# Scanning two states at a time on VectorE in a Mamba, attention and experts kernel

## The chip, the cores and the metric

The kernel runs on one core of one Trainium2 chip. The metric is the device time of one execution in microseconds (us); runs are compared by their medians. Five engines work side by side, each through its own queue in order: TensorE (PE in the profile, with its weight loads as PEld), VectorE (DVE), ScalarE (ACT), GpSimd (POOL) and SyncE (SP), which here only issues transfers.

## The reference

The input is `x` of shape (4, 128, 64, 64) in float32. Layer 0 normalises it by groups, then by channels, applies a 3x3 convolution per channel with a small residual branch, splits the 128 channels into four chunks of 32 and sends each through a Mamba block with 64 inner channels and 16 states per channel. A projection and a residual follow. Layer 1 is attention with four heads over the 4096 tokens of an image, then a choice of two out of eight experts per token. What matters here is the recurrence of the Mamba block:

```python
delta = jax.nn.softplus(dt @ dt_proj_w.T + dt_proj_b)
A = -jnp.exp(A_log)
dA = jnp.exp(delta[..., None] * A)
dBu = delta[..., None] * Bm[:, :, None, :] * xin[..., None]

def step(h, inp):
    dA_t, dBu_t, C_t = inp
    h = dA_t * h + dBu_t
    y = jnp.einsum('bdn,bn->bd', h, C_t)
    return (h, y)
```

For every image, inner channel and each of the 16 states n, h runs over the 4096 positions; y is the sum over n of C times h.

## The kernel before, in words

**Tiles.** An image is cut into 8 blocks of 512 positions (BLK). Two chunks of the 128 channels are handled together: 2 x 64 inner channels fill the 128 partitions. So an image has 8 blocks x 2 halves (index p) x 16 states (index n), and four images give 1024 units (b, i, p, n). Each is one state of one half block: a product `h = B * du`, a scan over 512 columns with the decay `da`, and a product `hc = C * h`, all on VectorE, in `scan` (L747 to L758). The scan begins at the value that the same state had at the end of the block before (`states`, L730), or at zero in the first block.

**The main loop** (L1244 to L1298) makes one unit per pass; a pass is called a slot. What it issues, in this order, on queues that keep the program's order (`Queue`, L439; all records so carry line 445):

1. `flush` issues stores that are due. Then the transfer that spreads B and C of the unit three slots on over the partitions (`fetched`, L732, tile `rows`, four buffers, 512 KB) from the DRAM tile `bcd`, which `inputs` (L679) wrote.
2. ScalarE copies the last column of the slot before's h into `states` (L1253), then makes the decay of the unit two slots on (`decayed`, L742, three buffers).
3. The next step of attention (`attention_groups`): TensorE makes the scores of two key tiles (`sc`), ScalarE their exponentials (`pT`).
4. VectorE's scan of the unit. In the first 128 slots (`ALONE`, L1241) its `hc` goes to the sum as it is. Later GpSimd adds the `hc` of an odd state to that of the even one (L1269) and the pair goes as one.
5. Two lanes of other work, X and Y, move on by two stages each (`advance`, L1158). A lane is a list of generators whose stages each issue a few instructions, so that normalisation, convolution, projections, the inputs of later scans (Y), the closing of a block (`closed`, L790) and the experts (`finished`, L1031) lie between scans. The order within the slot: second half of X's step, first of Y's, sums of `hc`, second of Y's, attention's weighted values of the slot before (`weighted`, TensorE tile `av`), first of X's.
6. The sum over states is made by TensorE in one PSUM buffer `y`: plain matmuls with the identity in the first 128 slots, later transposing matmuls (`turned_on`, L766), whose result ScalarE copies (`yT`) and TensorE turns back (`turned_back`, L781).

If a unit's inputs are not made in time, `until` (L1186) runs the lanes ahead. After the last scan the loop goes on with attention and experts alone. On image 0 the 3x3 convolution is done on TensorE, on later images on VectorE (`conv`, L609, tile `cm`).

Of the kernel before, what the change touches and what calls it, by code (L numbers as in the profile page):

```python
# [9 lines left out]
F32 = mybir.dt.float32  # L10
F32R = mybir.dt.float32r
# [25 lines left out]
def conv_mamba_attn_moe_kernel(ctx: ExitStack, tc: tile.TileContext, t: dict):  # L37
# [450 lines left out]
        return ps_work.tile(shape or [P, BLK], F32, tag=f"work{lane}", name=f"ps_{lane}")  # L488

    def tmp(lane, name, shape=None):  # L490
        return side.tile(shape or [P, BLK], F32, tag=f"tmp{lane}", name=name, bufs=4)

    def transposed(lane, src):
        ps = work(lane)
# [184 lines left out]
    def inputs(b, i, p):  # L679

        xn, pairs = xn_of[b, i], pairs_of[b, i]
        r = slice(DI * p, DI * p + DI)
        while held:
            yield
            yield
        held.add("in")
        ps = work("Y")
        summed(ps, [(inxc[:, j, :], pairs[:, p, 2 * j : 2 * j + BLK]) for j in range(2)])
        pz = work("X")
        mm(pz, inz[r, :], xn[r, 3 : 3 + BLK])  # L690
# [12 lines left out]
        held.clear()  # L703
        bc = tmp("Y", "bc")[0:DI, :]
        scalar.copy(bc, pb[0:DI, :])
        bcd = dram.tile([2, NST, 2 * BLK], F32, name="bcd", bufs=4)
        send(bcd.rearrange("c n (k q) -> (c n k) q", k=2), bc)

        e = tmp("Y", "e")
        scalar.activation(e, ps, AF.Abs, bias=dtb)  # L710
        scalar.activation(e, e, AF.Exp, scale=-1.0)
        ln = tmp("Y", "ln")
        scalar.activation(ln, e, AF.Ln, bias=1.0)
        delta = mix.tile([P, BLK], F32, name="delta", bufs=2)
# [17 lines left out]
    def fetched(b, i, p, n):  # L732

        bcd = in_of[b, i, p][4]
        w = mix.tile([P, 2, BLK], F32, name="rows", bufs=4)
        sync.dma_start(
            out=w.rearrange("p k q -> p (k q)"),
            in_=bcd[:, n, :][None].to_broadcast([DI, 2, 2 * BLK]),
        )
        return w  # L740

    def decayed(b, i, p, n):  # L742
        da = mix.tile([P, BLK], F32, name="da", bufs=3)
        scalar.activation(da, in_of[b, i, p][2], AF.Exp, scale=amat[:, n : n + 1])
        return da

    def scan(b, i, p, n, w, da):  # L747
# [12 lines left out]
    def scanned(b, i, p, y):  # L760
        xin, zs, delta, du, bcd = in_of.pop((b, i, p))
# [28 lines left out]
    def closed(b, i):  # L790
# [58 lines left out]
        for d, w, bias in ((kd, wkn, bkn), (qd, wqn, bqn)):  # L849
            ps = work("X")  # L850
            mm(ps, w, xa)
            yield
            hi = side.tile([P, BLK], F32R, name="hi", bufs=2)
            vector.tensor_scalar(hi, ps, bias, None, ALU.add)
            lo = side.tile([P, BLK], F32R, name="lo", bufs=2)
            vector.scalar_tensor_tensor(
                lo, ps, bias, hi.bitcast(F32), ALU.add, ALU.subtract
            )
            for half, w in enumerate((hi, lo)):
                w = w.bitcast(F32)  # L860
# [57 lines left out]
    def attention(b):  # L918
# [25 lines left out]
        for at, part in enumerate(parts):  # L944
# [9 lines left out]
            for g in range(0, NT * n, STEP):  # L954
# [9 lines left out]
                pTs = []  # L964
                for j in range(g, g + STEP):
                    sc = ps_sc.tile([P, 2, BLK], F32, name="sc")
                    for u in range(2):
# [4 lines left out]
                    pT = att.tile([P, 2, BLK], F32, name="pT", bufs=4)  # L972
                    scalar.activation(pT, sc, AF.Exp, scale=ATT_SCALE)
                    pTs.append((v[:, j // NT, j % NT, :], pT))
                yield (
                    b, q, h, pTs, first and g == 0, last and g + STEP == NT * n, prev, final,
                )

    sums, partial, total, inverse, later = [None], {}, {}, {}, deque()

    def weighted(group):
        b, q, h, pTs, first, last, prev, final = group
# [175 lines left out]
    def advance(lane, second):  # L1158
# [3 lines left out]
        while True:  # L1162
            if lane not in running:

                tasks = lanes[lane] if lanes[lane] or slot < len(units) else lanes["X"]
                if not tasks or not all(k in done for k in tasks[0][2]):
                    return False

                if (
                    tasks[0][0][0] == "out" and slot < len(units) + 4  # L1170
                    and not 2 <= slot % (2 * NST) < NST + 2
                ):
                    return False
# [68 lines left out]
    rows, decays, old, due, closing = {}, {}, None, deque(), deque()  # L1242
    even, y_of, waiting, slot = None, {}, None, 0
    while slot < len(units) or due or closing or waiting or left or later or lanes["X"] or running:  # L1244
        flush()

        for ahead in range(slot if slot == 0 else slot + 3, min(slot + 4, len(units))):
            until(("in", *units[ahead][:3]))
            rows[ahead] = fetched(*units[ahead])
        if old:  # L1250
            (b, i, p, n), h = old
            if i < NB - 1:
                scalar.copy(states[b % 2][:, p, n : n + 1], h[:, BLK - 1 : BLK])  # L1253
            old = None
        for ahead in range(slot if slot == 0 else slot + 2, min(slot + 3, len(units))):
            decays[ahead] = decayed(*units[ahead])
        group = next(groups, None)
        if slot < len(units):
            unit = units[slot]
            h, hc = scan(*unit, rows.pop(slot), decays.pop(slot))  # L1260
            old = unit, h
            b, i, p, n = unit
# [12 lines left out]
        while due and due[0][0] <= slot:  # L1275
            at, unit, term, first = due.popleft()
            b, i, p, n = unit
            if first:
                y_of[b, i, p] = ps_y.tile([P, BLK], F32, name="y")
            y, ends = y_of[b, i, p], n == NST - 1  # L1280
            if at <= ALONE:
                mm(y, ident, term, first, ends)
                if ends:
                    summed_up(b, i, p, y_of.pop((b, i, p)))
            else:
                turned_on(y, term, first, ends)
                if ends:
                    yT = mix.tile([P, BLK], F32, name="yT")
                    scalar.copy(yT, y_of.pop((b, i, p)))
                    closing.append((slot + 1, b, i, p, yT))  # L1290
        advance("Y", True)
        if waiting:
            weighted(waiting)
        waiting = group
# [31 lines left out]
def _laid_out(i):  # L1326
# [18 lines left out]
    wbc = np.zeros((P, 2, NST, 2), np.float32)  # L1345
    xdt, dtT = np.zeros((4, P), np.float32), np.zeros((4, P), np.float32)
    for c in range(2):
        d = slice(c, P, 2)
# [3 lines left out]
            inz[s, d] = c0["in_proj_w"][DI:].T  # L1352
            wout[d, p, s] = c0["out_proj_w"].T

        wbc[d, c] = c0["x_proj_w"][2:].reshape(2, NST, DI).transpose(2, 1, 0)
        xdt[2 * c : 2 * c + 2, d] = c0["x_proj_w"][:2]
        dtT[2 * c : 2 * c + 2, d] = c0["dt_proj_w"].T

# [53 lines left out]
```

## Time and profile before

| what | value |
| --- | --- |
| median of 3 runs | 5496.23 us (5489.41 to 5500.91) |
| the profiled execution's own time | 5490.03 us |
| its span in the trace | 5488.3 us |
| TensorE matmul busy | 4780.5 us, 87% |
| VectorE busy | 4404.5 us, 80% |
| ScalarE busy | 3923.3 us, 71% |
| GpSimd busy | 1981.4 us, 36% |
| 1024 scans | 1364.1 us (896 with a state) and 186.6 us (128 that begin at zero) |
| 1024 products h, 1024 products hc | 843.3 us and 882.4 us |

The profile is one execution recorded on the chip, with the start and length of each instruction. A group of instructions stands as engine, operation, tile written, tiles read and shape, followed by the count, the busy time in us, the mean in ns, the idle time of the engine just before them and what ended that idle time. Matmuls are pipelined, so that a busy TensorE is not a TensorE at its peak. Operations that can't start because another engine holds what they need may show this as a longer length, so a mean above the median is worth a look.

### The profile page before, as it was taken

The page shows a single profiled execution, that of the slowest core. Times are in us where ns is not written, and L with a number is a line of the kernel's source. Part 1 is how long each engine was busy: PE and PEld are TensorE (multiplying, and loading weights), DVE is VectorE, ACT ScalarE, POOL GpSimd, SP SyncE. Part 2 cuts the span into 40 slices and gives each one's busy share as a digit, 9 for nine tenths or more (in the row PEclk, how much of TensorE's full clock was granted, in tenths as well). Part 3 has the DMA queues.
Part 4 walks back from the last instruction along what each step waited for, and adds up shares of the span by engine and source line. Part 5 has one row for each costly group of instructions (what it writes and reads, how often), then busy time and mean ns, then how long its engine had stood idle before and what let it go on. Part 6 is the DMA issues. An engine that isn't in the chain of part 4 may idle for free.

```text
span 5488.3 us, 63616 instructions
## 1 busy us (share of the span) xinstructions
PE 4780.5 (87%) x18986; PEld 2159.0 (39%) x18986; DVE 4404.5 (80%) x6659; ACT 3923.3 (71%) x6045; POOL 1981.4 (36%) x1533
## 2 busy tenths in 40 slices
PE   4677798898988888898898898888889898999997
PEld 2223343443444443444444443344444443444443
DVE  4898888889888889988988888888989888871231
ACT  3455687788877777677877777777777777766553
POOL 2222345445433344344533434343443334420100
PEclk8778998999999999999999999999999999999998
DMA  3556566677656667666765666667765666765542
GB/s 98 173 178 195 194 216 229 223 233 254 219 197 206 226 206 244 221 225 220 252 214 196 221 209 233 237 202 240 250 207 200 209 225 196 249 200 167 168 148 68
DMA packets 451714, 1131.67 MB, mean 206 GB/s; under 512 B 51985, under 2 KB 135330, under 8 KB 451362
## 3 DMA queue, kind: packets, MB, share of 16 engines
q1 hardware_dynamic: 450194, 1126.74, 61.5%
q8 instruction: 153, 2.51, 0.2%
q14 instruction: 199, 1.63, 0.1%
q10 hardware_dynamic: 1168, 0.80, 0.1%
HBM read 967.12 MB, written 143.39 MB: 202 GB/s over the span
## 4 chain that ended last, share of the span: by engine, by line
PE 41%; DVE 31%; ACT 11%; issue 8%; DMA 7%; POOL 1%; SPq 0%; DVEq 0%; ACTq 0%; POOLq 0%
DVE h L445 17%; PE av L445 16%; PE sc L445 10%; PE ps_X L445 8%; PE ps_Y L445 5%; ACT pT L445 4%; DVE hc L445 3%; DMA ks<-kd 2%; PE y L445 2%; ACT xt L445 2%; DVE cm L445 2%; ACT L445 2%; DMA rows<-bcd 1%; DVE share L445 1%; DMA inv<-inverse 1%
## 5 line engine op out<-in xcount | busy, mean ns | idle before, releaser
L445 ACT ACTIVATE pT<-sc 128x1024 f32<-128x1024 f32 x2048 | 1983.1, 1022 | 976.0 <-PE sc L445 973.0
L445 PE MATMUL av<-pT,v 128*64 128x512 f32 x8192 | 2022.7, 615 | 7.3 <-ACT avs L445 7.1
L445 DVE TENSOR_TENSOR_SCAN h<-da,state,h 128x512 f32<-128x512 f32 x896 | 1364.1, 1522 | 100.7 <-ACT da L445 8.1
L445 PE MATMUL sc<-qs,ks 128*128 128x512 f32 x4096 | 1333.3, 447 | 116.1 <-ACT pT L445 60.1
L445 POOL TENSOR_TENSOR hc<-hc 128x512 f32<-128x512 f32 x448 | 677.6, 1513 | 1526.0 <-DVE hc L445 1354.4
L445 PEld LDWEIGHTS sc<-qs,ks 128*128 128x128 f32 x4096 | 728.1, 196 | 808.7 <-ACT pT L445 297.1
L445 DVE TENSOR_TENSOR hc<-rows,h 128x512 f32<-128x512 f32 x1024 | 882.4, 862 | 79.9 <-DVE h L445 2.7
L445 DVE TENSOR_TENSOR h<-rows,du 128x512 f32<-128x512 f32 x1024 | 843.3, 824 | 42.5 <-POOL du L445 25.6
L445 PEld LDWEIGHTS av<-pT,v 128*64 128x64 f32 x8192 | 506.0, 138 | 913.5 <-issue 880.9
L445 ACT ACTIVATE da<-delta,amat 128x512 f32<-128x512 f32 x1024 | 751.2, 734 | 16.7 <-DVE h L445 12.6
L445 ACT ACT_TABLE_LOAD x319 | 409.3, 1283 | 18.6 <-PE ps_Y L445 13.3
L445 POOL TENSOR_TENSOR rsY<-rsY,mhalf 128x4 f32<-128x4 f32 x100 | 139.9, 1399 | 575.1 <-DVE shiftY L445 574.1
L445 ACT COPY state<-h 128x1 f32<-128x1 f32 x896 | 177.2, 198 | 221.8 <-DVE h L445 221.4
L445 POOL TENSOR_TENSOR avs<-avs,prev 128x512 f32<-128x512 f32 x96 | 145.1, 1511 | 425.3 <-ACT avs L445 343.3
L445 PE MATMUL y<-ident,hc 128*128 128x128 f32 x1792 | 274.9, 277 | 7.0 <-POOL hc L445 7.0
L445 PEld LDWEIGHTS y<-ident,hc 128*128 128x128 f32 x1792 | 223.1, 142 | 106.4 <-issue 50.4
L445 DVE TENSOR_TENSOR share<-share,xf 128x1024 f32<-128x1024 f32 x128 | 174.5, 1363 | 105.0 <-DMA share<-sharesX 73.9
L445 PE MATMUL ps_X<-share,w_ew 128*128 128x512 f32 x432 | 224.4, 643 | 39.4 <-DVE share L445 39.4
L445 POOL TENSOR_TENSOR rsX<-rsX,mhalf 128x4 f32<-128x4 f32 x92 | 112.3, 1221 | 304.7 <-DVE shiftX L445 304.3
L445 POOL TENSOR_SCALAR du<-e 128x512 f32<-128x512 f32 x64 | 128.3, 2005 | 251.5 <-ACT e L445 251.5
L445 POOL TENSOR_TENSOR zs<-xin,zs 128x512 f32<-128x512 f32 x64 | 107.4, 1678 | 290.1 <-DVE xin L445 280.9
L445 PE MATMUL y<-hc,ident 128*128 128x512 f32 x256 | 169.4, 758 | 45.5 <-DVE hc L445 45.3
(239 smaller groups left out, 4832.2 us busy)
## 6 DMA issues: line engine op xcount, KB each, us to landing
rows<-bcd SPq DMA_DIRECT2D x1024, 512.0 KB
ks<-kd SPq DMA_DIRECT2D x192, 512.0 KB
qs<-qd SPq DMA_DIRECT2D x161, 512.0 KB
share<-sharesX SPq DMA_DIRECT2D x108, 512.0 KB
v<-vd SPq DMA_DIRECT2D x192, 256.0 KB
ks<-kd SPq DMA_DIRECT2D x128, 256.0 KB
avd<-avs SPq DMA_DIRECT2D x96, 256.0 KB
prev<-avd SPq DMA_DIRECT2D x96, 256.0 KB
```

The source lines that it names most:

```text
L445: return lambda *args, **kw: queued(op(*args, **kw))
```

## The change

A unit is now two neighbouring states, and there are 512 of them. It takes two slots, so that the number of slots and what the lanes and attention do in each stay what they were.

- The scan runs over one row of 1025 columns: 512 of the first state, one column between them, 512 of the second. In the column between, the decay is a constant zero (written once into two standing decay tiles), and the driving term is the second state's value from the block before. The recurrence so forgets the first state and begins at that value. ScalarE writes it there (`carried`). The initial value of the scan is always read from `states`, which GpSimd fills with zeros at the start of each image.
- In the even slot VectorE makes the product `h` of both states (1024 columns, `driven`) and the scan. In the odd slot, after lane X's step, it makes the product `hc` of both (`read`).
- `bcd` is laid out so that a fetched tile holds B of both states or C of both, not B and C of one. The count and the size of the transfers stay. C of the next unit is fetched in the even slot and B of the unit after it in the odd one.
- A unit's decays are made one in each of the two slots before it. ScalarE saves both last columns with one copy at the end of the even slot (`kept`).
- The first 64 slots, not 128, send `hc` to the sum without GpSimd's addition; there, too, the transposing form is used. Buffers: two of h and hc with both states in each, two of the decay.
- The two halves `hi` and `lo` of keys and queries use lane X's common temporaries, now six. The exponentials are issued by a function of their own at the same place.

```diff
@@
-        return side.tile(shape or [P, BLK], F32, tag=f"tmp{lane}", name=name, bufs=4)
+        return side.tile(
+            shape or [P, BLK], F32, tag=f"tmp{lane}", name=name, bufs=6 if lane == "X" else 4
+        )
@@
-        bcd = dram.tile([2, NST, 2 * BLK], F32, name="bcd", bufs=4)
-        send(bcd.rearrange("c n (k q) -> (c n k) q", k=2), bc)
+        bcd = dram.tile([2, NST // 2, 2, 2 * BLK], F32, name="bcd", bufs=4)
+        send(bcd.rearrange("c n k (m q) -> (c n k m) q", m=2), bc)
@@
+    decays = [mix.tile([P, 2, BLK + 1], F32, name=f"da{k}") for k in range(2)]
+    for k in range(2):
+        gpsimd.memset(decays[k][:, 0, BLK:], 0.0)
...
+    def carried(unit):
+
+        b, i, p, n = unit
+        if (i, p, n) == (0, 0, 0):
+            gpsimd.memset(states[b % 2], 0.0)
+        h = mix.tile([P, 2, BLK + 1], F32, name="h", bufs=2)
+        scalar.copy(h[:, 0, BLK:], states[b % 2][:, p, n + 1 : n + 2])
+        return h
+
+    def kept(unit, h):
+        b, i, p, n = unit
+        if i < NB - 1:
+            scalar.copy(states[b % 2][:, p, n : n + 2], h[:, :, BLK - 1])
+
+    def driven(unit, h, w):
+        b, i, p, n = unit
         du = in_of[b, i, p][3]
-        h = mix.tile([P, BLK], F32, name="h", bufs=3)
-        vector.tensor_mul(h, w[:, 0, :], du)
+        vector.tensor_mul(h[:, :, 0:BLK], w, du[:, None, :].to_broadcast([P, 2, BLK]))
+
+    def scan(unit, h, da):
+
+        b, i, p, n = unit
+        h, da = (a.rearrange("p k q -> p (k q)")[:, 0 : 2 * BLK + 1] for a in (h, da))
         vector.tensor_tensor_scan(
-            out=h, data0=da, data1=h, initial=0.0 if i == 0 else states[b % 2][:, p, n : n + 1],
+            out=h, data0=da, data1=h, initial=states[b % 2][:, p, n : n + 1],
             op0=ALU.mult, op1=ALU.add,
         )
-        hc = mix.tile([P, BLK], F32, name="hc", bufs=5)
-        vector.tensor_mul(hc, w[:, 1, :], h)
-        return h, hc
+
+    def read(h, w):
+        hc = mix.tile([P, 2, BLK], F32, name="hc", bufs=2)
+        vector.tensor_mul(hc, w, h[:, :, 0:BLK])
+        return hc
@@
-    units = [(b, i, p, n) for b, i in blocks for p in range(2) for n in range(NST)]
-
-    ALONE = NB // 2 * 2 * NST
...
+    units = [(b, i, p, n) for b, i in blocks for p in range(2) for n in range(0, NST, 2)]
+    END = 2 * len(units)
+
+    ALONE = NB // 2 * NST
...
+        fetch((at + 2, 0) if odd else (at + 1, 1))
+        unit = units[at] if at < len(units) else None
+        prepared(at + 1, odd)
         group = next(groups, None)
+        if group:
+            group = exponentials(group)
+        if unit and not odd:
+            h = h_of.pop(at)
+            driven(unit, h, rows.pop((at, 0)))
+            scan(unit, h, decays[at % 2])
+        advance("X", True)
+        if unit and odd:
+            hc = read(h, rows.pop((at, 1)))
             if slot < ALONE:
-                due.append((slot + 1, unit, hc, n == 0))
-            elif n % 2 == 0:
-                even = hc
+                due.append((slot + 1, unit, 0, hc[:, 0, :], False))
+                due.append((slot + 2, unit, 1, hc[:, 1, :], ends(unit)))
             else:
-                gpsimd.tensor_add(even, even, hc)
-                due.append((slot + 2, unit, even, n == 1))
-        advance("X", True)
+                gpsimd.tensor_add(hc[:, 0, :], hc[:, 0, :], hc[:, 1, :])
+                due.append((slot + 2, unit, 0, hc[:, 0, :], ends(unit)))
         advance("Y", False)
...
         advance("Y", True)
+        if unit and not odd:
+            kept(unit, h)
         if waiting:
             weighted(waiting)
         waiting = group
```

Here `prepared(ahead, k)` makes decay k of a unit and, with the second one, its carry.

More of the change, by code (lines that the diff above doesn't have):

```diff
@@ L730, in conv_mamba_attn_moe_kernel, with fetched @@
     states = [mix.tile([P, 2, NST], F32, name=f"state{k}") for k in range(2)]
-    def fetched(b, i, p, n):
-        bcd = in_of[b, i, p][4]
+    decays = [mix.tile([P, 2, BLK + 1], F32, name=f"da{k}") for k in range(2)]
+    for k in range(2):
+        gpsimd.memset(decays[k][:, 0, BLK:], 0.0)
+    def fetched(unit, k):
+        b, i, p, n = unit
         w = mix.tile([P, 2, BLK], F32, name="rows", bufs=4)
         sync.dma_start(
-            out=w.rearrange("p k q -> p (k q)"),
-            in_=bcd[:, n, :][None].to_broadcast([DI, 2, 2 * BLK]),
-        )
-        return w
@@ L742, in decayed @@
[L742 to L747, printed above, removed]
+            out=w.rearrange("p m q -> p (m q)"),
+            in_=in_of[b, i, p][4][:, n // 2, k, :][None].to_broadcast([DI, 2, 2 * BLK]),
+        )
+        return w
+    def decayed(unit, da, k):
+        b, i, p, n = unit
+        scalar.activation(
+            da[:, k, 0:BLK], in_of[b, i, p][2], AF.Exp, scale=amat[:, n + k : n + k + 1]
+        )
@@ L749, in scan @@
+    def carried(unit):
[10 more added lines that the diff above has]
+    def driven(unit, h, w):
+        b, i, p, n = unit
         du = in_of[b, i, p][3]
-        h = mix.tile([P, BLK], F32, name="h", bufs=3)
@@ L751, in scan @@
-        vector.tensor_mul(h, w[:, 0, :], du)
+        vector.tensor_mul(h[:, :, 0:BLK], w, du[:, None, :].to_broadcast([P, 2, BLK]))
+    def scan(unit, h, da):
+        b, i, p, n = unit
+        h, da = (a.rearrange("p k q -> p (k q)")[:, 0 : 2 * BLK + 1] for a in (h, da))
         vector.tensor_tensor_scan(
-            out=h, data0=da, data1=h, initial=0.0 if i == 0 else states[b % 2][:, p, n : n + 1],
+            out=h, data0=da, data1=h, initial=states[b % 2][:, p, n : n + 1],
             op0=ALU.mult, op1=ALU.add,
@@ L852, in closed @@
             yield
[L853 to L858, printed above, removed]
+            hi, lo = tmp("X", "hi"), tmp("X", "lo")
+            vector.tensor_scalar(hi.bitcast(F32R), ps, bias, None, ALU.add)
+            vector.scalar_tensor_tensor(lo.bitcast(F32R), ps, bias, hi, ALU.add, ALU.subtract)
             for half, w in enumerate((hi, lo)):
-                w = w.bitcast(F32)
                 if len(d.shape) == 4:
@@ L963, in attention @@
                         ahead = load(nxt, qs if nxt[:2] == (q, h) and not nxt[5] else None)
-                pTs = []
+                scs = []
                 for j in range(g, g + STEP):
@@ L971, in attention, with exponentials @@
                         )
-                    pT = att.tile([P, 2, BLK], F32, name="pT", bufs=4)
-                    scalar.activation(pT, sc, AF.Exp, scale=ATT_SCALE)
-                    pTs.append((v[:, j // NT, j % NT, :], pT))
+                    scs.append((v[:, j // NT, j % NT, :], sc))
                 yield (
-                    b, q, h, pTs, first and g == 0, last and g + STEP == NT * n, prev, final,
+                    b, q, h, scs, first and g == 0, last and g + STEP == NT * n, prev, final,
                 )
     sums, partial, total, inverse, later = [None], {}, {}, {}, deque()
+    def exponentials(group):
+        pTs = []
+        for v, sc in group[3]:
+            pT = att.tile([P, 2, BLK], F32, name="pT", bufs=4)
+            scalar.activation(pT, sc, AF.Exp, scale=ATT_SCALE)
+            pTs.append((v, pT))
+        return *group[:3], pTs, *group[4:]
     def weighted(group):
@@ L1163, in advance @@
             if lane not in running:
-                tasks = lanes[lane] if lanes[lane] or slot < len(units) else lanes["X"]
+                tasks = lanes[lane] if lanes[lane] or slot < END else lanes["X"]
                 if not tasks or not all(k in done for k in tasks[0][2]):
@@ L1169, in advance @@
                 if (
-                    tasks[0][0][0] == "out" and slot < len(units) + 4
+                    tasks[0][0][0] == "out" and slot < END + 4
                     and not 2 <= slot % (2 * NST) < NST + 2
@@ L1238, in conv_mamba_attn_moe_kernel @@
     groups = attention_groups()
-    units = [(b, i, p, n) for b, i in blocks for p in range(2) for n in range(NST)]
-    ALONE = NB // 2 * 2 * NST
-    rows, decays, old, due, closing = {}, {}, None, deque(), deque()
-    even, y_of, waiting, slot = None, {}, None, 0
-    while slot < len(units) or due or closing or waiting or left or later or lanes["X"] or running:
-        flush()
[L1247 to L1256, printed above, removed]
-        group = next(groups, None)
[L1258 to L1262, printed above, removed]
+    units = [(b, i, p, n) for b, i in blocks for p in range(2) for n in range(0, NST, 2)]
@@ new lines, in conv_mamba_attn_moe_kernel, with fetch, prepared @@
+    END = 2 * len(units)
+    ALONE = NB // 2 * NST
+    rows, due, closing, y_of = {}, deque(), deque(), {}
+    h_of, slot = {}, 0
+    def fetch(*wanted):
+        for ahead, k in wanted:
+            if ahead < len(units):
+                until(("in", *units[ahead][:3]))
+                rows[ahead, k] = fetched(units[ahead], k)
+    def prepared(ahead, k):
+        if ahead < len(units):
+            decayed(units[ahead], decays[ahead % 2], k)
+            if k:
+                h_of[ahead] = carried(units[ahead])
@@ new lines, in ends @@
+    def ends(unit):
+        return unit[3] == NST - 2
+    waiting = None
+    while slot < END or due or closing or waiting or left or later or lanes["X"] or running:
+        at, odd = divmod(slot, 2)
+        flush()
+        if slot == 0:
+            fetch((0, 0), (0, 1), (1, 0))
+            prepared(0, 0)
+            prepared(0, 1)
+        fetch((at + 2, 0) if odd else (at + 1, 1))
+        unit = units[at] if at < len(units) else None
+        prepared(at + 1, odd)
+        group = next(groups, None)
+        if group:
[7 more added lines that the diff above has]
+            hc = read(h, rows.pop((at, 1)))
@@ L1275, in conv_mamba_attn_moe_kernel @@
         while due and due[0][0] <= slot:
-            at, unit, term, first = due.popleft()
-            b, i, p, n = unit
+            _, (b, i, p, n), k, term, done_with = due.popleft()
+            first = n == 0 and k == 0
             if first:
                 y_of[b, i, p] = ps_y.tile([P, BLK], F32, name="y")
[L1280 to L1290, printed above, removed]
+            turned_on(y_of[b, i, p], term, first, done_with)
+            if done_with:
+                yT = mix.tile([P, BLK], F32, name="yT")
+                scalar.copy(yT, y_of.pop((b, i, p)))
+                closing.append((slot + 1, b, i, p, yT))
         advance("Y", True)
+        if unit and not odd:
+            kept(unit, h)
         if waiting:
@@ L1344, in _laid_out @@
     wout = np.zeros((P, 2, P), np.float32)
-    wbc = np.zeros((P, 2, NST, 2), np.float32)
+    wbc = np.zeros((P, 2, NST // 2, 2, 2), np.float32)
     xdt, dtT = np.zeros((4, P), np.float32), np.zeros((4, P), np.float32)
@@ L1353, in _laid_out @@
             wout[d, p, s] = c0["out_proj_w"].T
-        wbc[d, c] = c0["x_proj_w"][2:].reshape(2, NST, DI).transpose(2, 1, 0)
+        wbc[d, c] = c0["x_proj_w"][2:].reshape(2, NST // 2, 2, DI).transpose(3, 1, 0, 2)
         xdt[2 * c : 2 * c + 2, d] = c0["x_proj_w"][:2]
```

## The prediction

> **What bounds the kernel now.** I read the shares of busy time first, because two engines compete for the bound, and then the chain that ended last.
>
> ```profile
> PE 4780.5 (87%) x18986; PEld 2159.0 (39%) x18986; DVE 4404.5 (80%) x6659; ACT 3923.3 (71%) x6045; POOL 1981.4 (36%) x1533
> PE 41%; DVE 31%; ACT 11%; issue 8%; DMA 7%; POOL 1%; SPq 0%; DVEq 0%; ACTq 0%; POOLq 0%
> ```
>
> The reader sees that neither TensorE (PE) nor VectorE (DVE) is the bound alone. An average hides stages, so next I took busy time by stretch. Scans start between 97.5 us (first) and 4895.7 us (last). One pass of the main loop, a slot, holds one scan. In the trace scan 128 starts at 577.4 and scan 288 at 1282.9 us, so the four rows are slots 0 to 127 (stage A), 128 to 287 (B), 288 to 1023 (C) and the tail without scans (D). Columns: length, PE, PEld, DVE, ACT, POOL busy, clock, DMA share, GB/s.
>
> ```profile
> 97.50:577.40 479.90, 350.77 (x842) 138.66 (x843) 420.00 (x603) 265.22 (x489) 125.12 (x105) 0.79 0.55 183
> 577.40:1282.90 705.50, 616.96 (x2499) 277.96 (x2499) 616.90 (x821) 555.80 (x854) 324.35 (x236) 0.94 0.66 220
> 1282.90:4895.70 3612.80, 3225.42 (x13354) 1484.17 (x13352) 3192.95 (x4683) 2767.32 (x4281) 1471.84 (x1107) 0.96 0.66 222
> 4895.70:5488.30 592.60, 547.72 (x2184) 239.30 (x2180) 150.31 (x425) 310.49 (x384) 41.94 (x44) 0.95 0.41 136
> ```
>
> A slot takes 3.75, 4.41 and 4.91 us in A, B and C. VectorE's 4.34 us of C is not all of its load: about 0.1 us in front of every scan and 0.08 in front of every hc product is idle time with almost no releaser named (70.4 + 7.2 + 57.8 us in C, 0.18 us per slot), the step from a result to its reader. With that VectorE is taken 3.48, 4.04 and 4.52 us per slot, TensorE 2.74, 3.86 and 4.38. A is VectorE's, C is nearly shared. In C each waits for the other; the waits of C:
>
> ```profile
> DVE res L445 <- PE ps_X L445: 106.6, 40, 7.0
> PE ps_X L445 <- DVE aT L445: 75.6, 21, 5.6
> PE ps_X L445 <- DVE prX L445: 65.4, 18, 4.6
> ACT state L445 <- DVE h L445: 73.0, 49, 3.0
> ```
>
> TensorE's lane work waits for VectorE's lane work that stands behind the scan in VectorE's queue. So VectorE's time is worth something in C, but not one for one.
>
> Last, the scan itself, one unstalled state, and the stalls (start, length):
>
> ```profile
> 2613.14 0.69 DVE L445 TENSOR_TENSOR h<-rows,du 128x512 f32<-128x512 f32 x1
> 2613.93 1.28 DVE L445 TENSOR_TENSOR_SCAN h<-da,state,h 128x512 f32<-128x512 f32 x1
> 2615.25 0.69 DVE L445 TENSOR_TENSOR hc<-rows,h 128x512 f32<-128x512 f32 x1
> 2615.86 0.74 DVE L445 TENSOR_SCALAR hi<-ps_X,w_bqn 128x512 fp32r<-128x512 f32 x1
> ...
> 2602.56 1.61 POOL L445 TENSOR_TENSOR hc<-hc 128x512 f32<-128x512 f32 x1 [0.95 <-DVE hc L445]
> 2603.13 2.13 DVE L445 TENSOR_TENSOR_SCAN h<-da,state,h 128x512 f32<-128x512 f32 x1
> ```
>
> From start to start one state occupies 0.79 + 1.32 + 0.61 = 2.72 us. A scan that meets a running GpSimd add takes 2.13 instead of 1.28 us. Medians and means of the three groups, and of the one operation with 1024 columns that the kernel already has:
>
> ```profile
> L445 DVE TENSOR_TENSOR_SCAN h<-da,state,h x896: 1282/1284/2395, 201.2 to 4895.7; 128x512 f32<-128x512 f32 x180
> L445 DVE TENSOR_TENSOR h<-rows,du x1024: 621/684/1784, 96.7 to 4894.9; 128x512 f32<-128x512 f32 x171
> L445 DVE TENSOR_TENSOR share<-share,xf x128: 1211/1221/2001, 1426.9 to 5479.7; 128x1024 f32<-128x1024 f32 x128
> L445 DVE TENSOR_TENSOR hc<-rows,h 128x512 f32<-128x512 f32 x1024 | 882.4, 862 | 79.9 <-DVE h L445 2.7
> ```
>
> (The first three give shortest, median and longest ns; the last busy us and the mean, 862 ns against a median of 693, so the difference is stalls.)
>
> **What the Trainium skill says.** "VectorE: DVE Perf Modes", the section on the perf-mode tier table: an fp32 product of two SBUF tensors runs at one element per cycle, with no faster mode. The trace agrees: 512 further columns cost 1221 - 684 = 537 ns. "DVE: opcode table, instruction layouts, handler registers and perf-mode slots", section 6: the built-in scan runs at half that throughput. The trace fits: 1284 ns is 2 x 537 plus 210 fixed. "SBUF — State Buffer", section "Who interferes with whom": a VectorE operation with two SBUF inputs and a GpSimd operation that reads SBUF exclude each other for the whole instruction. The 2.13 us scan above agrees. "Trainium Kernel Development and Optimization", section "Performance Expectations", warns that matmul busy time is a bad measure of how full TensorE is; so 4.38 us may overstate it, which I keep as a rival.
>
> **The change part by part.** *VectorE.* Two states take 2 x 2.72 = 5.44 us now. The new h product costs 0.79 + 0.54 = 1.33, the new hc product 0.61 + 0.54 = 1.15. No scan of 1025 columns is in the trace. Lower end: 513 more columns at two cycles, 513 x 2 x 1.049 = 1.08, so 1.32 + 1.08 = 2.40; upper end: no fixed part at all, 2.64. Nothing says that it gets below the lower end, whose fixed part is inferred from the product. I take 2.40, since its rate is what the page states. Sum 4.88, a saving of 0.56 us per pair, 0.28 per slot (0.16 at the upper end). The zero column is the 1025th and costs nothing else. The products' layout (a row pitch of 513) is not in the trace; I bound hc between 1.15 and the old 2 x 0.61, and take 1.15.
>
> *Stalls.* The pairwise GpSimd add stays, one per pair from slot 128 on, and each can hold one VectorE operation for some 0.85 us. Fewer but longer operations could meet it more or less often; bounds plus or minus 0.1 us per slot, value zero. But the bound ALONE falls from 128 to 64 slots: slots 64 to 127 get 32 GpSimd adds that they did not have, 32 x 0.85 = 27 us of VectorE in stage A.
>
> *ScalarE.* 896 state copies of 198 ns become 448 two-column ones plus 512 carries: 64 more, 13 us, beside the 23% of C in which ScalarE is idle (2767 of 3613 us busy); zero. Without that cover it would cost those 13 us. Two-column copies are not in the trace (198 to 396 ns); still hidden. The wait of the copy for the scan comes once per pair, in the even slot. Queued behind it are the second decay, the carry and the next exponentials, for which TensorE's score buffers wait. The decay has 0.73 us of work and the whole hc product in the odd slot ahead of its scan: no cost taken, up to 0.1 us per slot as bound.
>
> *TensorE and the y sum.* 128 plain 512-column products in A become transposing ones plus eight turns back, on an engine busy 73% of A: zero. In the first 64 slots the next y's first term now stands right behind the turn back in the single y buffer, and waits for VectorE to read it: four times, some 3 us (a scan and a product), 10 us at most with half of it hidden; I take 6.
>
> *DMA.* The row fetches stay 1024 of 512 KB, one per slot, three slots ahead of use, on SP's queue in the same place. A fetch into a reused buffer waits for the last product that read it: the h product for B rows, the hc product for C rows, both in the slot before, as now; zero. The send of bcd keeps size and place. hi and lo, and the position of the exponentials, move no instruction on an engine's queue; zero.
>
> *What becomes of it.* A: 128 x 0.28 = 36 less 27 less 6 = 3 us. B: VectorE falls to 4.04 - 0.28 = 3.76, under TensorE's 3.86. Today a slot is 0.37 us longer than its fuller engine; that stays, so 3.86 + 0.37 = 4.23, and 160 x 0.18 = 29 us. C: VectorE falls to 4.24, TensorE's 4.38 is next. Overhang 4.91 - 4.52 = 0.39, slot 4.77, and 736 x 0.14 = 103 us. D: no scans, zero. Sum 135 us. The profiled execution took 5490.03 us, its span 5488.3; it becomes about 5355. The median of the runs shown is 6 us above it, so I name 5361.
>
> **The rivals.** *VectorE's time counts in full.* For it: TensorE's busy time may be inflated, and in C TensorE waits for aT, prX and share products. Against it: the 106.6 us for which VectorE waits for ps_X. Then 896 x 0.28 = 251 plus 3, giving 5242.
>
> *It is mostly absorbed.* TensorE is already the bound in most slots, or the scan comes out at its upper end (0.16 per slot). Half of B and C: 66 us, giving 5430; less with stalls, to 5480.
>
> *Slower: bunched VectorE work holds TensorE in even slots.* Now 2.72 us plus stalls stand before each slot's lane work; then 1.33 + 2.40 = 3.73 in the even slot and nothing before lane X in the odd one. That is 1.0 us more in the even slot. If all of it reaches the in-order TensorE queue, and the odd slot can give back only TensorE's present slack, 4.91 - 4.38 = 0.53, a pair loses 0.47: 368 x 0.47 = 173 less 32 gives about 5640. It decides once more than 0.53 of that 1.0 us arrives at TensorE. Against it: VectorE has only 1.15 us of scan work in the odd slot and can start the next pair early.
>
> **How the numbers follow.** Forecast, 5300 to 5420: 0.50. In full, 5230 to 5300: 0.15. Absorbed, 5420 to 5485: 0.17. Within 0.2% (11 us, about what a measurement of this kernel can tell from no change): 0.04. Slower: 0.14. So faster 0.82. The range 5240 to 5470 leaves out the slower case, no change and the rim of the absorbed one, about 0.2. Both ends hold the bounds above: the stalls' 0.1 us is 90 us over B and C.
>
> **What would show it.** Right: 512 scans near 2.4 us median and about 1.22 us for both products; VectorE busy near 4404 - 250 to 290; slots of C near 4.77 us; the tail still about 590 us; waits of ps_X for aT and prX smaller, those of VectorE for ps_X larger. Wrong: scan or products with longer medians, means much above the medians (stalls grew), idle time of ScalarE in front of the state copy above 150 us, or TensorE waiting for lane X work in even slots.

## The result and the profile after

The changed kernel takes 5487.11 us at the median of 14 runs (5472.36 to 5493.63), the kernel before 5497.68 us in the same rounds (5486.38 to 5508.94). The ratio is 0.9982, its 95% interval 0.9974 to 0.999. That is 10 us, where 135 were forecast. The profiled execution took 5488.16 us, its span 5486.3.

VectorE's work fell by more than forecast, yet the time stayed. Part 1 of the page after:

```profile
PE 4717.2 (86%) x19146; PEld 2166.4 (39%) x19146; DVE 4014.9 (73%) x5123; ACT 3932.9 (72%) x6117; POOL 2416.2 (44%) x1571
```

VectorE is busy 390 us less (4404.5 before), in 1536 fewer instructions. The same four stretches, cut at the scans of the same slots (columns as before):

```profile
99.70:583.60 483.90, 283.30 (x990) 152.87 (x990) 395.21 (x412) 263.95 (x498) 215.59 (x137) 0.71 0.54 182
583.60:1283.60 700.00, 613.38 (x2508) 278.06 (x2507) 542.07 (x581) 557.17 (x870) 378.57 (x237) 0.95 0.66 222
1283.60:4890.80 3607.20, 3229.64 (x13351) 1476.05 (x13348) 2899.91 (x3578) 2775.50 (x4327) 1760.76 (x1109) 0.96 0.66 222
4890.80:5486.30 595.50, 550.82 (x2190) 240.50 (x2188) 152.76 (x425) 311.22 (x384) 42.97 (x45) 0.95 0.41 136
```

Stage A takes 4 us more, B 5.5 less, C 5.6 less, the tail 3 more. In C VectorE gives up 293 us of work and the slot falls from 4.91 to 4.90 us. The three operations (shortest, median and longest ns):

```profile
L445 DVE TENSOR_TENSOR h<-rows,du x512: 1206/1220/2323, 98.3 to 4889.5; 128x1024 f32<-128x1024 f32 x171
L445 DVE TENSOR_TENSOR_SCAN h<-da,state,h x512: 2353/3172/3457, 99.7 to 4890.8; 128x1025 f32<-128x1025 f32 x171
L445 DVE TENSOR_TENSOR hc<-rows,h x512: 1154/1220/2318, 102.1 to 4894.2; 128x1024 f32<-128x1024 f32 x171
```

Unstalled, the operations are as long as the forecast took them: the shortest long scan has 2353 ns, and the products' median is 1220. But most long scans were held up: their median is 3172 ns. What grew besides is VectorE's idle time for lane X, and with it TensorE's for `lo` and `share`. (In lane X, `hi` and `lo` are the halves of keys and queries, `stX` the statistics of a normalisation, `prX` the router's scores, `share` an input of the experts and `res` their sum; `ps_X` is what TensorE hands over.) Some of the waits in stage C of the changed kernel (us in total, times, longest):

```profile
DVE res L445 <- PE ps_X L445: 130.2, 54, 3.9
DVE stX L445 <- PE ps_X L445: 109.9, 23, 4.9
DVE hi L445 <- PE ps_X L445: 98.9, 20, 6.8
DVE prX L445 <- PE ps_X L445: 48.8, 22, 3.9
PE ps_X L445 <- DVE share L445: 62.7, 28, 3.9
PE ps_X L445 <- DVE lo L445: 62.5, 23, 3.0
```

In C before, `res` waited 106.6 us, and `hi` and `prX` do not stand in VectorE's list of the nine longest. The others, before:

```profile
DVE stX L445 <- PE ps_X L445: 43.1, 22, 2.0
PE ps_X L445 <- DVE share L445: 39.4, 24, 2.2
PE ps_X L445 <- DVE lo L445: 24.0, 25, 1.6
```

TensorE's waits in C for `aT` and `prX` fell, as the forecast had it, from 75.6 to 31.0 and from 65.4 to 3.9 us, 106 us together. But those for `share`, `lo`, ScalarE's `xt` and GpSimd's `hc` rose by 110 us. So TensorE stood idle for 378 us of C, where it had been 387.

How a wait for lane X works is seen in one place of the time line. In the kernel before, VectorE first, then TensorE:

```profile
2606.80 0.72 DVE L445 TENSOR_TENSOR h<-rows,du 128x512 f32<-128x512 f32 x1
2607.62 1.28 DVE L445 TENSOR_TENSOR_SCAN h<-da,state,h 128x512 f32<-128x512 f32 x1
2608.94 1.59 DVE L445 TENSOR_TENSOR hc<-rows,h 128x512 f32<-128x512 f32 x1
2610.46 0.74 DVE L445 TENSOR_SCALAR hi<-ps_X,w_bkn 128x512 fp32r<-128x512 f32 x1
```

```profile
2601.91 1.24 PE L445 MATMUL ps_X<-ident,xt 128*128 128x128 f32 x4
...
2607.21 1.13 PE L445 MATMUL ps_X<-xa,w_wkn 128*128 128x512 f32 x2 [0.48 <-ACT xa L445]
...
2617.44 1.16 PE L445 MATMUL ps_X<-w_wv,xa 128*128 128x128 f32 x8 [1.49 <-DVE lo L445]
```

VectorE does a state's three operations while `ps_X` is made, and `hi` begins without idle time. The same place of the same block in the changed kernel:

```profile
2597.60 1.21 DVE L445 TENSOR_TENSOR h<-rows,du 128x1024 f32<-128x1024 f32 x1
2598.92 2.36 DVE L445 TENSOR_TENSOR_SCAN h<-da,state,h 128x1025 f32<-128x1025 f32 x1
2606.93 0.75 DVE L445 TENSOR_SCALAR hi<-ps_X,w_bkn 128x512 fp32r<-128x512 f32 x1 [5.66 <-PE ps_X L445]
...
2608.39 1.32 DVE L445 TENSOR_TENSOR hc<-rows,h 128x1024 f32<-128x1024 f32 x1
...
2613.09 2.35 DVE L445 TENSOR_TENSOR_SCAN h<-da,state,h 128x1025 f32<-128x1025 f32 x1
2615.36 0.72 DVE L445 TENSOR_SCALAR hi<-ps_X,w_bqn 128x512 fp32r<-128x512 f32 x1
2616.11 0.75 DVE L445 SCALAR_TENSOR_TENSOR lo<-ps_X,w_bqn,hi 128x512 fp32r<-128x512 f32 x1
```

```profile
2599.46 1.48 PE L445 MATMUL ps_X<-ident,xt 128*128 128x128 f32 x4 [0.29 <-ACT xt L445]
...
2605.77 1.12 PE L445 MATMUL ps_X<-xa,w_wkn 128*128 128x512 f32 x2 [0.39 <-ACT xa L445]
...
2616.92 0.58 PE L445 MATMUL ps_X<-w_wv,xa 128*128 128x128 f32 x1 [2.95 <-DVE lo L445]
```

The scan ends at 2601.28. VectorE's next instruction in the odd slot is lane X's `hi`, whose input TensorE makes from 2605.77 on. So VectorE stands still for 5.66 us, though the hc product behind `hi` has had all it needs since 2601.28. That product, the next h product and the next scan then come late, the next `hi` and `lo` stand behind them, and now TensorE waits 2.95 us. The time saved on VectorE is spent in idle time in front of one instruction, and a later instruction is late all the same.

### The profile page after: what moved, and what is told of

The parts are those of the page before. It is cut to its first block, busy times and chain, and to the rows that moved or that the text cites. A ratio compares the mean times of both kernels' runs of the same rounds, so it can differ in the third digit from the quotient of the medians.

```text
span 5486.3 us, 61283 instructions
## 1 busy us (share of the span) xinstructions
PE 4717.2 (86%) x19146; PEld 2166.4 (39%) x19146; DVE 4014.9 (73%) x5123; ACT 3932.9 (72%) x6117; POOL 2416.2 (44%) x1571
## 5 line engine op out<-in xcount | busy, mean ns | idle before, releaser
L445 DVE TENSOR_TENSOR_SCAN h<-da,state,h 128x1025 f32<-128x1025 f32 x512 | 1484.1, 2899 | 161.8 <-ACT h L445 113.4
L445 POOL TENSOR_TENSOR hc<-hc 128x512 f32<-128x512 f32 x480 | 902.3, 1880 | 1342.6 <-DVE hc L445 1269.9
L445 DVE TENSOR_TENSOR h<-rows,du 128x1024 f32<-128x1024 f32 x512 | 720.2, 1407 | 40.2 <-POOL du L445 25.7
L445 DVE TENSOR_TENSOR hc<-rows,h 128x1024 f32<-128x1024 f32 x512 | 705.0, 1377 | 30.9 <-DVE h L445 23.4
L445 PE MATMUL y<-ident,hc 128*128 128x128 f32 x2176 | 357.8, 293 | 92.0 <-POOL hc L445 48.6
L445 PEld LDWEIGHTS y<-ident,hc 128*128 128x128 f32 x2176 | 289.1, 152 | 228.7 <-issue 76.8
L445 ACT COPY state<-h 128x2 f32<-128x2 f32 x448 | 88.5, 198 | 316.1 <-DVE h L445 315.9
L445 POOL TENSOR_SCALAR du<-e 128x512 f32<-128x512 f32 x64 | 204.0, 3188 | 114.2 <-ACT e L445 114.0
L445 ACT ACTIVATE xt<-ps_Y,shiftY,rsY 128x128 f32<-128x128 f32 x380 | 143.2, 463 | 101.0 <-POOL shiftY L445 94.0
L445 DVE TENSOR_TENSOR res<-res,ps_X 128x512 f32<-128x512 f32 x108 | 73.3, 679 | 173.3 <-PE ps_X L445 173.0
```

Of the source, the lines that this page charges most:

```text
L445: return lambda *args, **kw: queued(op(*args, **kw))
```

## The experiments

Four theories. O: the order in odd slots, lane X's step in front of ready scan work, loses the gain. B: bunching; h product and scan in a row hold lane X up in even slots. P: the pace of TensorE and ScalarE; VectorE's time has no price. S: ScalarE's copy of the end states (`kept`) waits for the scan, with decay, exponentials and the carry (the column between the two states, which ScalarE writes) queued behind. Every run stands beside the kernel before in its own rounds; its median there was 5493 to 5500 us.

**The hc product first.**

```diff
-        advance("X", True)
         if unit and odd:
             hc = read(h, rows.pop((at, 1)))
+        advance("X", True)
+        if unit and odd:
```

> The changed kernel with one thing moved: in odd slots the product hc of both states goes in front of lane X's step on VectorE, not behind it. Theory O (order): VectorE's freed time is lost because in odd slots it sits idle for lane X's result from TensorE (hi, stX, prX, res after ps_X) with the ready hc product queued behind; then the waits of VectorE on ps_X fall and the time drops by 40 to 120 us from 5487. Theory P (pace): TensorE and ScalarE set the slot and VectorE's time is worth nothing; 5487 within 12 us. Theory S (ScalarE's in-order copy of the end states delays carry, decay and exponentials): no change, 5487 within 12 us. Theory B (bunching: the h product and the scan, 3.7 us in a row, hold up lane X in even slots): little change, as the even slot stays as it is, within 25 us.

5389.07 us, ratio to the kernel before 0.9801 (0.9788 to 0.9815): 98 us faster than the changed kernel by moving one instruction. O holds; P and S would have left the time where it was, and B within 25 us. Two other readings of the move fall short. That the sum over states gets its `hc` sooner shows no effect: TensorE waited for it in front of `y` for 84 us in the changed kernel and 81 here. And the long scan is held up less (median 2356 ns, not 3172), but VectorE is busy only 48 us less by all of it, which at the prices found below (0.20 to 0.54) makes 10 to 26 of the 98 us.

**The state copy later.**

```diff
-        if unit and not odd:
+        if unit and odd:
             kept(unit, h)
```

> The changed kernel with ScalarE's copy of both end states moved from the end of the even slot to the end of the odd one, so that nothing of the odd slot (second decay, carry, exponentials) stands behind a wait for the scan. Theory S: ScalarE's 316 us of waiting in front of the state copy and VectorE's 113 us for the carry go, and 50 to 100 us of time with them. Theories O, P and B: the waits go but the time stays within 15 us of 5487.

5497.84 us, 0.9991 (0.9982 to 0.9999). The wait it aimed at went, the other one stayed:

```profile
ACT state L445 <- DVE h L445: 51.1, 20, 5.1
DVE hi L445 <- PE ps_X L445: 134.9, 30, 6.9
```

The copy waited 315.9 us in the changed kernel; 265 us of it go and the time doesn't fall. S falls as far as the copy goes; VectorE's wait for the carry, which S also wanted gone, fell only from 113.4 to 92.2 us. A long wait on an engine with time to spare is no loss by its length alone.

**The kernel before with half of the hc product.** The product is made for 256 of 512 columns, so half of the sum over states is left out. The five hc tiles stand for the whole run and hold zeros in the other half.

```diff
-        vector.tensor_mul(hc, w[:, 1, :], h)
+        vector.tensor_mul(hc[:, 0 : BLK // 2], w[:, 1, 0 : BLK // 2], h[:, 0 : BLK // 2])
```

> The kernel before, with VectorE's product hc made for the first 256 of 512 columns alone; the other half of the five standing hc tiles holds zeros (half of the sum over states is left out). It takes about 0.27 us per slot from VectorE, as much as the change does, and leaves order and every other engine's instructions as they are. Theory P: the time stays at 5497 within 15 us, VectorE's time has no price. Theories O, B and S: VectorE's time is worth about half, as forecast: 1024 x 0.27 x 0.5 = 138 us, that is 5360 within 50 us.

5402.19 us, 0.9821 (0.9807 to 0.9834). VectorE is busy 4120.5 us, 284 less, and 98 us come out: a price of 0.34, inside the range of the second expectation, but less than the half that was forecast. P falls as the sole cause.

**Two scans, spread over both slots.** Products of 1024 columns, scans of 512, no carry column; the state copy stands at the end of the odd slot. The cut shows the main loop alone.

```diff
         if unit and not odd:
             driven(unit, h, rows.pop((at, 0)))
-            scan(unit, h, decays[at % 2])
-        advance("X", True)
+            scan(unit, h, decays[at % 2], 0)
         if unit and odd:
+            scan(unit, h, decays[at % 2], 1)
             hc = read(h, rows.pop((at, 1)))
+        advance("X", True)
```

> The changed kernel with products of 1024 columns, but two scans of 512 columns, the first behind the h product in the even slot, the second in the odd slot in front of the hc product, both ahead of lane X's step; no carry column is written and the state copy stands at the end of the odd slot. VectorE's work is spread evenly over slots (about 2.65 and 2.47 us) and lane X always comes after the scan work, as before; two of the three savings stay (about 0.16 us per slot). Theories O and B: faster than the changed kernel, 5400 to 5440. Theory P: 5490 within 12 us. Theory S: gain of the copy alone, as with the copy moved alone.

5368.75 us, 0.9767 (0.9754 to 0.978), faster than either theory asked for. VectorE, then TensorE, in the same place of the same block as above:

```profile
2540.93 4.28 DVE L445 TENSOR_TENSOR_SCAN h<-da,state,h 128x512 f32<-128x512 f32 x2
2545.41 1.23 DVE L445 TENSOR_TENSOR hc<-rows,h 128x1024 f32<-128x1024 f32 x1 [0.20 <-POOL y L445]
2546.55 0.75 DVE L445 TENSOR_SCALAR hi<-ps_X,w_bkn 128x512 fp32r<-128x512 f32 x1
```

```profile
2539.69 1.09 PE L445 MATMUL ps_X<-ident,xt 128*128 128x128 f32 x3
...
2544.84 1.12 PE L445 MATMUL ps_X<-xa,w_wkn 128*128 128x512 f32 x2 [0.48 <-ACT xa L445]
...
2554.09 1.16 PE L445 MATMUL ps_X<-w_wv,xa 128*128 128x128 f32 x8 [1.05 <-DVE lo L445]
```

While TensorE makes `ps_X`, VectorE does the second scan and the hc product; `hi` begins with no wait. From the start of the transposes to that of the values matmul TensorE needs 14.4 us here, 15.5 in the kernel before and 17.5 in the changed kernel.

**Order alone, with even load.** The kernel with two scans, lane X's step first in odd slots.

```diff
+        advance("X", True)
         if unit and odd:
             scan(unit, h, decays[at % 2], 1)
             hc = read(h, rows.pop((at, 1)))
-        advance("X", True)
```

> As the kernel with two scans of 512 columns spread over both slots (5369 us), but in odd slots lane X's step goes on VectorE in front of the second scan and the hc product. Load per slot stays even, so bunching can't matter; only the order changes. Theory O (order): the ready scan work waits behind lane X's operations for TensorE, and the gain goes again: 5450 to 5550. Theory B (bunching of h product and scan in even slots was what cost the gain): 5370 within 20 us.

5545.71 us, 1.0094 (1.0077 to 1.0111): 177 us slower with the same operations and slots of equal load. This tells O from B.

**Order alone, in the kernel before.** On VectorE nothing but the order changes. On GpSimd the pairwise addition also moves, behind what lane X gives GpSimd in that step.

```diff
+        if slot % 2:
+            advance("X", True)
         if slot < len(units):
...
-        advance("X", True)
+        if slot % 2 == 0:
+            advance("X", True)
```

> The kernel before with only the order changed: in odd slots lane X's step goes on VectorE in front of the three scan operations, in even slots behind them as it was. No operation is added or taken away. Theory O: VectorE idles in odd slots for lane X's inputs with 2.7 us of ready work queued behind, so slower than 5497: 5570 to 5700. Theory B, where order has no price of its own: 5497 within 25 us.

5745.59 us, 1.0456 (1.0442 to 1.0471), 248 us slower, more than O expected. Nothing of the changed kernel's scan is in this one, so O needs neither the pairs nor the long scan:

```profile
DVE stX L445 <- PE ps_X L445: 173.5, 33, 6.5
PE ps_X L445 <- DVE lo L445: 110.5, 31, 7.2
```

(66.7 and 35.4 us in the kernel before.)

The place looked at above occurs 32 times in a run. From the start of the keys' matmul to that of the values' (worked out from the traces) it takes 9.7 us on average before and 11.8 with X first; 11.0 in the changed kernel and 9.5 with the hc product first; 9.0 with two scans and 11.3 with X first there.

**The h product a slot ahead, one scan.** All three savings, even slots of one scan, odd slots of two products, lane X last.

```diff
+            if slot == 0:
-            driven(unit, h, rows.pop((at, 0)))
+                driven(unit, h, rows.pop((at, 0)))
             scan(unit, h, decays[at % 2])
-        advance("X", True)
         if unit and odd:
             hc = read(h, rows.pop((at, 1)))
+            if at + 1 < len(units):
+                driven(units[at + 1], h_of[at + 1], rows.pop((at + 1, 0)))
+        advance("X", True)
```

> The changed kernel with its one scan of 1025 columns, but the h product of the next unit is made one slot earlier, behind the hc product in the odd slot, and lane X's step comes behind both. The even slot then has 2.4 us of scan work, the odd one 2.5, all three savings stay and lane X is always behind the scan work. Theories O and B: at or under the two scans' 5369 us, about 5345, since VectorE has 0.12 us less per slot than there, worth a third to a half: 40 to 60 us, less what the shorter lead of the fetched B rows costs. If the scan of 1025 columns has a price of its own (ScalarE's carry in front of it, GpSimd held off for 2.4 us at a time): 5380 to 5400, near the kernel with the hc product first.

5376.05 us, 0.9782 (0.9768 to 0.9795). VectorE is busy 3980.6 us here against 4163.3 with two scans, 183 us less, for no gain; the time lies between the two expectations. It is 13 us under the hc product first (5389), which is what the even load brings here, net: the waits for the carry and for fetched rows in front of VectorE grew at the same time (178.6 to 306.4 us and 17.4 to 70.5). The wait for the carry, which ScalarE writes behind the second decay, is now VectorE's longest. The next two kernels ask whether such waits are the reason.

**ScalarE's part earlier.** The kernel above, with

```diff
+            prepared(1, 0)
...
-        prepared(at + 1, odd)
+        if not odd:
+            prepared(at + 1, 1)
...
-        if unit and not odd:
+        if unit and odd:
             kept(unit, h)
+            prepared(at + 2, 0)
```

> As the kernel with the h product one slot ahead (5376 us), with ScalarE's part earlier: the second decay and the carry at the start of the even slot before, not of the odd slot, the first decay of the unit after it at the end of the odd slot, the state copy in front of it. If the one scan of 1025 columns gains nothing over two scans because VectorE now waits for ScalarE (306 us in front of the scan for the carry), those waits fall under 100 us and the time drops by 15 to 50, to 5326 to 5361, under the two scans' 5369. If VectorE's time has run out of worth at this level, as TensorE and lane X set the rest: 5370 within 10 us though the waits go.

5396.15 us, 0.9824 (0.9811 to 0.9838). The wait for the carry fell to 14.4 us, yet the time rose by 20. Both expectations missed.

**Both rows fetched in the even slot**, and 128 slots without GpSimd's addition; the rest as in the kernel above.

```diff
-        fetch((at + 2, 0) if odd else (at + 1, 1))
+        if not odd:
+            fetch((at + 1, 1), (at + 2, 0))
```

> The same, with both rows fetched in the even slot, so that the B rows again have three slots until they are used, and the stretch without GpSimd's addition at 128 slots. The 70 us that VectorE waited for fetched rows fall under 10, the longer stretch is worth 2 to 5 us: 5 to 25 us under the kernel beside it if these waits were on the path, equal within 8 us if not.

5409.51 us, 0.9846 (0.9833 to 0.986). The h product waited 63.5 us for rows in the kernel above. That wait is gone from the list, yet it is slower again by 13 us: no gain from these waits either. A miss. Two things changed at once here; the longer stretch alone is the next run.

**The stretch without GpSimd's addition at 128 slots**, on the kernel with two scans.

```diff
-    ALONE = NB // 2 * NST
+    ALONE = NB // 2 * 2 * NST
```

> As the kernel with two scans (5369 us), with the stretch in which TensorE sums hc without GpSimd's addition at 128 slots again, as in the kernel before, not 64. The forecast priced the 32 additions of slots 64 to 127 at 27 us (32 x 0.85 us of stalled VectorE). If that holds: 5342 within 8 us. If these stalls are mostly hidden: 5360 to 5369, since slots 64 to 127 took 4.14 us each in the changed kernel against 4.02 before, 8 us in all.

5367.14 us, 0.9765 (0.9751 to 0.9778), against 5368.75: no difference that can be told. The stalls that the 32 additions cause are mostly hidden.

**No GpSimd addition at all**, on the kernel with two scans.

```diff
-    ALONE = NB // 2 * NST
+    ALONE = END
```

> As the kernel with two scans (5369 us), without GpSimd's addition of the two hc halves in any slot: TensorE sums each of them (128-column transposing matmuls, four more per slot and so about 0.2 us more per slot on TensorE). If GpSimd's hold[...] and its late additions cost more than that: 5280 to 5350. If TensorE's time sets the slot: slower, 5450 to 5560, as 0.2 us over 900 slots is 180 us at most.

5414.97 us, 0.9846 (0.9829 to 0.9862): 46 us slower. VectorE loses 261 us of busy time (188 of it stalls of scans and products) and TensorE takes 161 us more. Slower, as the second expectation had it, but by about half of its least.

**Two scans with half of the hc product** (half of the sum over states left out, as above).

```diff
-        vector.tensor_mul(hc, w, h[:, :, 0:BLK])
+        vector.tensor_mul(hc[:, :, half], w[:, :, half], h[:, :, half])
```

> As the kernel with two scans (5369 us), with the hc product made for 256 of each 512 columns alone (the other half of two standing hc tiles holds zeros, so half of the sum over states is left out). It takes another 0.27 us per slot from VectorE. If VectorE's time is still worth a third, as in the kernel before (98 us for 284 us): 5270 to 5300. If it has run out of worth, because TensorE, its score buffers and the lanes' chains set the slot: 5350 to 5375. The two kernels with ScalarE's part or the fetches earlier speak for the second.

5314.17 us, 0.967 (0.9656 to 0.9683). VectorE is busy 280 us less and 55 us come out, between both expectations: its time still has a price, 0.20 now.

In one table: VectorE's busy time, its waits for `ps_X` in front of `hi`, `stX`, `res` and `prX` together, and TensorE's in front of `ps_X` for `lo` and `share` together, over the whole span:

| kernel | median us | VectorE busy | VectorE waits for lane X | TensorE waits |
| --- | --- | --- | --- | --- |
| before | 5497.68 | 4404.5 | 239 | 75 |
| before, X first | 5745.59 | 4431.1 | 442 | 188 |
| changed | 5487.11 | 4014.9 | 515 | 149 |
| state copy later | 5497.84 | 4021.9 | 525 | 147 |
| hc product first | 5389.07 | 3966.7 | 366 | 71 |
| two scans | 5368.75 | 4163.3 | 248 | 52 |
| two scans, X first | 5545.71 | 4186.8 | 469 | 163 |
| h product ahead | 5376.05 | 3980.6 | 230 | 44 |

Each pair that differs in order alone (before, changed against hc product first, two scans) has longer waits and a longer time with lane X first. Across kernels the waits do not rank the times: VectorE waits longer with the hc product first than before, and has the more time to spare.

## Why the prediction was wrong

**What held.** VectorE's three operations: the scan took 2353 ns unstalled, both products 1220, as the sum had them (2.40 from start to start, 1.22). The tail took 595.5 us (592.6 before). TensorE's waits for `aT` and `prX` fell, VectorE's for `ps_X` rose. ScalarE's copies, the transfers and the transposing sums, all put at zero, were not tested one by one in the changed kernel; VectorE waited 113 us there for the carry.

**What was mis-sized.** VectorE was to be busy 250 to 290 us less and was 390 less. Means minus unstalled lengths give the stalls: 559 us before (scans 213 and 30, h 143, hc 173), 455 after (279, 96, 80). So the three operations lost 263 us of work, as forecast, and 104 us of stalls. The forecast put the stalls at zero with bounds of 0.1 us per slot, and 104 us in 1024 slots is at that bound. It was the products that met fewer; the scans' stalls grew, and their median of 3172 ns is one of the signs that the forecast had named for being wrong. The 27 us for GpSimd's additions in slots 64 to 127 were far too much: on the kernel with two scans the longer stretch without them changed 2 us.

**The step that failed** is the one under "What becomes of it": "Today a slot is 0.37 us longer than its fuller engine; that stays". That is said of B; for C the same step kept an overhang of 0.39 us and set it on TensorE's 4.38, a slot of 4.77. Measured, the slot is 4.90 us over TensorE's 4.39, an overhang of 0.51, against 0.53 over TensorE before: TensorE was as idle as ever, so next to nothing of VectorE's 0.28 us per slot came out. The step took the two engines as loads that share a slot. They are queues in order, and the change altered what stands behind what. The slower rival even wrote of "nothing before lane X in the odd one", and counted it as room to give time back. It was the loss: with nothing in front of it, lane X's step is reached before TensorE has made its input, and the ready hc product waits behind it. Moving that product back to the front gave 98 of the missing 125 us; the reverse order alone cost 177 us with even slots and 248 us in the kernel before.

**The rivals.** The slower rival, bunching in even slots, had the right place for TensorE's wait (`lo`, in the even slot) but the wrong cause: with the order right, the bunched kernel is 13 and 20 us from the two even ones, in differences that hold other changes too. "Mostly absorbed" named the size without a mechanism. The signs listed for a wrong forecast included the state copy above 150 us. It came (316 us) and misled: taking it away did not help.

**What VectorE's time is worth** is not one number: 0.54 for the step from the kernel before to two scans (131 us for 241), though that also has fewer ScalarE copies; 0.34 for half the hc product before; 0.20 after two scans. The forecast's half was right for the first of these only. Even the hc product first, which mends the order, gains 111 us for 438 us of VectorE's time, 0.25. That it comes within 28 us of the forecast's 5361 is in part luck: a price put too high, on a saving put too low.

**What stays open.** That loss and gain came out almost equal is not explained; nothing shows that it is more than chance. Why one scan of 1025 columns, with its order mended, gains nothing over two scans of 512 with 183 us more VectorE work is open too: the waits for the carry and for the rows were taken away and the time rose. GpSimd is busy 2473 us there against 2302, so longer operations may hold it off for longer, but that was only argued. What holds the kernels with ScalarE's part and the fetches earlier back by 20 and 13 us was not found. A lead for the first: TensorE's waits in front of `ps_X` for what ScalarE makes there (`xt`, `xa`, `xf`) grew from 83 to 148 us when ScalarE's queue was reordered. Whether that is the reason was not tested.

## What to carry to other kernels

Before counting on time taken from an engine, look at what its queue holds next: an instruction that waits for another engine blocks ready work behind it, and a saved microsecond in front of such a wait can turn into idle time. When work is merged into fewer, longer operations, put the pieces that are ready in front of those that wait for the other engine, and check by moving the order alone, with the operations unchanged (98, 177 and 248 us here). A wait is worth removing only if its removal moves the time; here 265 us of ScalarE's waiting went for nothing.

## What the runs showed of the hardware

513 more columns lengthened the scan from 1284 to 2353 ns, 2.08 ns per column with 217 ns fixed, where 512 more columns lengthened the product h from 684 to 1220 ns, 1.05 ns per column. The Trainium skill, "DVE: opcode table, instruction layouts, handler registers and perf-mode slots", section 6, gives the built-in scan half throughput, and the long form agrees.

Half as many products of twice the length had 176 us of stalls, where there were 316. The scans' stalls did not fall with their number: 243 us for 1024 short ones, 279 for 512 long ones. Part of these stalls is due to GpSimd's additions: in the kernel with two scans the scans and products have 472 us of stalls, and 284 when TensorE takes over the additions.

Some of GpSimd's own operations took longer in the changed kernel. This one had a mean of 2005 ns before and has 3188 after; that VectorE's longer operations hold it up is likely, but no run shows it by itself:

```profile
L445 POOL TENSOR_SCALAR du<-e 128x512 f32<-128x512 f32 x64 | 204.0, 3188 | 114.2 <-ACT e L445 114.0
```
